# A graph attention layer on one core: another order for the lead-in and for the last places

## The chip, the cores and the metric

The kernel runs on one core of a Trainium2 chip. Its time is the device time of one execution in microseconds; every kernel is run several times, and the median counts. A profiled execution leaves a trace with the start and duration of each instruction on TensorE (PE, and PEld for its weight loads), VectorE (DVE), ScalarE (ACT), GpSimd (POOL) and SyncE (SP), and of the transfers. SP, ACT and POOL each issue transfers, and each has a queue of its own: q1 is SP's, q10 ACT's, q0 POOL's.

## The reference

One layer of attention over a graph, with a residual and a layer norm. There are 16 batches of 1024 nodes with 512 features, 8 heads of 64, and one adjacency matrix for all batches. It is sparse: node i has few neighbours, and the fewer the larger i is.

```python
def reference(x, adj, Wq, bq, Wk, bk, Wv, bv, Wo, bo):   # x (16,1024,512), adj (1024,1024) of 0 and 1
    q = (x @ Wq + bq).reshape(b, n, 8, 64)
    k = (x @ Wk + bk).reshape(b, n, 8, 64)
    v = (x @ Wv + bv).reshape(b, n, 8, 64)
    scores = jnp.einsum('bqhd,bkhd->bhqk', q, k) / 8.0
    scores = scores + (1.0 - adj)[None, None] * -1e9
    out = jnp.einsum('bhqk,bkhd->bqhd', softmax(scores), v).reshape(b, n, 512)
    return layernorm(x + out @ Wo + bo)
```

## The kernel before

**The sparse form.** The 1024 nodes are sorted by their number of neighbours into 8 tiles of 128 queries. For each tile the kernel knows how many keys a query has at most, and handles them in blocks: in a block every one of 128 rows has one query and one key. POOL gathers the 128 rows of k and v by an indirect transfer (`kvg`, L1230), DVE multiplies them with the queries (`qk`, L1251) and sums over each head (`s`, L1255), ACT takes the exponential (L1266), and ACT or DVE multiplies it with v (`pv`, L1276 and L1280). The blocks of one query are added on DVE (L1292) or, for the tiles with many keys, by TensorE with a matrix of zeros and ones (`sum`, L1301 and L1302). `normalise` divides (`o`, L1322), TensorE transposes (`poT`, L1336), ACT copies (`oT`, L1340), and `finish` multiplies with Wo (`po`, L790), adds the residual, and normalises the row (L1099 to L1121). A spilled tile's oT is stored and loaded back as `oTs`.

**The dense part.** For every pair of tiles TensorE transposes x (`pxT`, L748) and computes q (`pq`, L790, four passes of 128x512 per tile) and k and v together. For k and v of a pair, seven products stand in place of eight (L947: `x`, `p6`, `p7`, `z`, `p4`, of which x and z are built up in two steps), with sums T1 to T4 of the weights' quarters (B11, B21, B12, B22; L382 to L387 on DVE) and sums of x (L774 to L777). Only the first pair of batch 0 takes k and v in the plain way (`pk` and `pv`, L919), since T1 to T4 aren't there yet. The results are stored to memory, k and v by L840 and q by L822, from SP's queue. DVE adds up all v of a batch (`vsum`, a tile with one buffer; L851 for the first pair, L854 for the others), TensorE makes their mean (`pm`, L858), ACT copies it (L862) and SP stores it (L864): a query without neighbours gets the mean.

**The order.** The program is written out by a loop over places n, from −39 to the last block, and each engine keeps the order in which its instructions were written. At each place come the steps of the blocks n to n+8, then what `later(k, fn)` has put down for this place, then units of TensorE work: `fronts` is the list of dense units, each with a cost in microseconds, and as many are taken as a credit allows that grows by a share per place. `urgent` holds units that go in ahead of the list. At the end of a place `preps` take a step: generators, each started at a place of its own (`prep`), whose `yield` means "go on at the next place".

**The lead-in.** The places below 0 are the lead-in. `loads` issues the weights on ACT's queue, then zeros for the rows that nobody writes; `ranks` loads adj on POOL's queue, counts the neighbours on DVE (L451, L452) and ACT (L453), ranks the nodes (L485) and scatters them into `order` (L479); `pranks` (L497) is a transpose of the ranks. `checks` and `estimate` look at the degrees (`est`, L672; `poff`, L675), `more_ranks` makes tables for the merged tiles (L552 to L578) with small copies on SP's queue (L539 and L543), `lookups` translates keys to places. `bias_setup` makes the norms of the biases (L399 to L405), then the bias as columns, `bvb` (L415), and `pb3` (L419), which folds bv into bo. The first three tiles of x are loaded by SP before the loop, and each transposed tile issues the load of the third tile after it (`load_x`, L741). The units of TensorE begin with

```python
fronts += transpose_x(0, 0) + transpose_x(0, 1)
```

and go on with q of both tiles, the next two transposes, pk and pv.

**The last places.** While the last three blocks come, TensorE's list may hold a `finish` of a tile (eight passes with a bias row, L1078) between the last sums.

Of the kernel before, what the change touches and what calls it, by code (L numbers as in the profile page):

```python
# [10 lines left out]
F32 = mybir.dt.float32  # L11
# [3 lines left out]
OP = mybir.AluOpType  # L15
# [46 lines left out]
MORE_RANKS_AT = -12  # L62
# [11 lines left out]
P = 128  # L74
# [103 lines left out]
def kernel(  # L178
# [36 lines left out]
    nc = tc.nc  # L215
# [32 lines left out]
    def broadcast(t, v):  # L248
        nc.scalar.dma_start(t, bass.AP(tensor=v.tensor, offset=v.offset, ap=[[0, P], [1, D]]))

    def load_w(t, w):
        nc.scalar.dma_start(t, w.rearrange("(c p) e -> p c e", p=P))

    with ExitStack() as main:
# [6 lines left out]
        def fill_psum(name):  # L261
            return psum.tile([P, HALF], F32, tag="fill", name=name, bufs=4)
# [12 lines left out]
        nc.gpsimd.iota(placed, pattern=[[P, max(BLOCKS)]], base=1, channel_multiplier=1, allow_small_or_imprecise_dtypes=True)  # L275
        query = one.tile([P, NT], F32, name="query")
# [79 lines left out]
        def loads():  # L356

            load_w(W["q"], wq)
            broadcast(bq_bc, bq)
            nc.vector.tensor_scalar(bq_bc, bq_bc, scale, None, op0=OP.mult)  # L360
            yield

            B12[0] = work.tile([P, 2, D], F32, tag="kv", name="b12", bufs=5)
            load_w(B11, wk[0:HD2, :])
            load_w(B21, wk[HD2:D, :])
            load_w(B12[0], wv[0:HD2, :])
            load_w(B22, wv[HD2:D, :])
# [3 lines left out]
            for rows in solo_rows + pair_rows:  # L371
                for r in range(N, rows.shape[0], N + 1):
                    nc.scalar.dma_start(rows[r:r + 1, 0:D], zeros[0:1, 0:D])
            for i in range(1, ROWS):
                nc.scalar.dma_start(q_rows[i][ds(ONE_KEY * P, P), :], zeros[:, 0:D])
                if i % B >= PAIRED_FROM and not merged(i):
                    nc.scalar.dma_start(q_rows[i][0:P, :], zeros[:, 0:D])
            left = P - 8 * (B - PAIRED_FROM)
            nc.scalar.dma_start(more_rows[P - left:, :], zeros[0:left, 0:D])
# [14 lines left out]
        def bias_setup():  # L394
            bk_bc = work.tile([P, D], F32, tag="y", name="bk_bc", bufs=Y_BUFS)
            broadcast(bk_bc, bk)
            yield
# [8 lines left out]
            yield  # L406
            pb = fill_psum("pb")
# [8 lines left out]
            yield  # L416
# [25 lines left out]
        def later(k, fn):  # L442
            plan.setdefault(now[0] + k, []).append(fn)
# [11 lines left out]
        def ranks():  # L455
# [40 lines left out]
            pr = fill_psum("pranks")  # L496
            nc.tensor.transpose(pr[0:NT, 0:P], rank, ident)  # L497
# [5 lines left out]
            yield  # L503
            yield
# [31 lines left out]
        def more_ranks():  # L536
# [15 lines left out]
            nc.vector.tensor_scalar(steps, place[:, 0:n], float(spare), query[:, 0:1], op0=OP.mult, op1=OP.is_le)  # L552
            nc.vector.tensor_reduce(eighths, steps, axis=AX.X, op=OP.add)
            nc.vector.tensor_scalar(steps, place[:, 0:n], float(2 * spare), query[:, 0:1], op0=OP.mult, op1=OP.is_le)
# [23 lines left out]
            nc.vector.tensor_scalar(missing, missing, -NEG, None, op0=OP.mult)  # L578
            yield
# [7 lines left out]
        def lookups():  # L587
# [4 lines left out]
            for i, group in enumerate(groups):  # L592
                while i >= NT and i < len(groups) - 1 and len(SHORT) + i - NT not in listed:
                    yield
# [22 lines left out]
        shifts, looked = [], []  # L617
# [13 lines left out]
        def edges(t):  # L631
# [41 lines left out]
            yield  # L673
# [133 lines left out]
        def pair(b, j):  # L807
# [25 lines left out]
            def send(i):  # L833
# [8 lines left out]
                if R["sent"] == 2:  # L842
                    later(1, add_v)
                    if j == NT // 2 - 1:
                        later(2, lambda: urgent.append(mean_pe))
# [67 lines left out]
            if (b, j) == (0, 0):  # L913
# [12 lines left out]
                units = q0 + q1 + xt  # L926
# [55 lines left out]
            def s(i):  # L982
                return lambda: SX[b, j][i - 1]
# [3 lines left out]
            units += unit("p6", s(2), T2, True, out_w, None)  # L987
            units += q0
# [452 lines left out]
        prep.setdefault(BIAS_AT, []).append(bias_setup())  # L1441
        prep.setdefault(CHECKS_AT, []).append(checks())
# [5 lines left out]
        with tc.manual_schedule():  # L1448

            fronts += transpose_x(0, 0) + transpose_x(0, 1)  # L1450
# [19 lines left out]
            while n < total or plan or rest or urgent or done or finishing or spilled or lone_tiles or not guarded:  # L1470
# [53 lines left out]
                while credit > 0 or urgent:  # L1524
# [9 lines left out]
                    units = finishing or fronts  # L1534
# [55 lines left out]
```

## Time and profile before

| what | value |
|---|---|
| median of five runs | 1891.6 us (1887.18 to 1895.26) |
| profiled execution | 1895.35 us, its span 1893.4 us |
| granted TensorE clock | 0.986 on average |
| busy: PE, DVE, ACT, POOL | 1819.9, 1700.2, 1531.7, 1281.2 us |
| PE busy in 0 to 100, 100 to 200, 200 to 300 us | 88.52, 91.84, 100.00 us |
| DVE busy in the same | 74.99, 84.53, 85.18 us |
| PE busy in 1850 to 1893.4 us | 24.75 us |
| bytes moved, mean rate | 544.63 MB, 288 GB/s |

The times of the views count from the start of the span. A line of the timeline gives the start, the duration, the engine, the line of the kernel, the operation with its output and inputs, how many of them follow each other, and in brackets the idle time before and what ended it. PE's clock is throttled by the chip: where the granted clock is below 1.00, the same pass takes up to twice as long.

### The profile page before, as it was taken

The numbers are of one execution on the slowest core, as the hardware profiler recorded it, in microseconds if no ns is written. First come the engines' busy times: TensorE is split into PE (matmuls) and PEld (weight loads), VectorE is DVE, ScalarE is ACT, GpSimd is POOL, SyncE is SP. The second block draws the span as 40 slices with busy tenths as digits, with TensorE's granted clock in tenths as the row PEclk, the third lists the DMA queues.
The fourth block names the chain that finished last, engine by engine and source line by source line (L and its number), as shares of the span: only waits on it lengthen the run. The fifth ranks groups of instructions, "written<-read, shape, count | busy, mean of one in ns | idle before, by whom it ended". The sixth has DMA issues, their size and how long they took to land. (4 is left out here: it accounts for less than half of the span.)

```text
span 1893.4 us, 25101 instructions
## 1 busy us (share of the span) xinstructions
PE 1819.9 (96%) x5149; PEld 879.3 (46%) x5149; DVE 1700.2 (90%) x3484; ACT 1531.7 (81%) x6016; POOL 1281.2 (68%) x1189
## 2 busy tenths in 40 slices
PE   7989999999999999999999999999999999999996
PEld 3434444444545454444445444444445444444442
DVE  6888889999999999899899989899999989997874
ACT  3628869979788988889797978889898989886794
POOL 1357766777677677758677677767766777656774
PEclk9989999999999999999999999999999999999997
DMA  7357786988888988888889898998889898989893
GB/s 279 119 167 230 227 311 228 317 291 293 302 291 312 315 313 290 314 287 299 306 294 330 274 332 276 301 310 305 304 306 328 291 348 307 318 288 344 328 314 119
DMA packets 188149, 544.63 MB, mean 288 GB/s; under 512 B 32602, under 2 KB 32622, under 8 KB 187986
## 3 DMA queue, kind: packets, MB, share of 16 engines
q0 software_dynamic: 116400, 382.82, 60.2%
q1 hardware_dynamic: 68510, 154.30, 21.9%
q10 hardware_dynamic: 3076, 5.82, 0.9%
q14 instruction: 120, 0.98, 0.2%
q8 instruction: 43, 0.70, 0.1%
HBM read 419.52 MB, written 144.34 MB: 298 GB/s over the span
## 5 line engine op out<-in xcount | busy, mean ns | idle before, releaser
L1276 ACT ACTIVATE pv<-kvg,pv 128x64 f32<-128x64 f32 x3432 | 864.7, 340 | 0.0
L1230 POOL DMA_INDIRECT kvg<-kv_pair,place_row x462 | 533.6, 1155 | 246.9 <-ACT pv L1276 66.4
L790 PE MATMUL po<-wo,oT 128*128 128x512 f32 x816 | 385.2, 603 | 0.8 <-ACT oT L1340 0.8
L790 PE MATMUL pq<-wq,xT 128*128 128x512 f32 x792 | 370.4, 599 | 0.2 <-DVE q L821 0.2
L1255 DVE TENSOR_REDUCE s<-qk 128x8 f32<-128x512 f32 x530 | 360.3, 680 | 7.5
L1251 DVE TENSOR_TENSOR qk<-qt,kvg 128x512 f32<-128x512 f32 x434 | 296.6, 683 | 26.2 <-DMA kvg<-kv_pair,place_row 26.2
L947 PE MATMUL x<-b,xT 128*128 128x512 f32 x504 | 238.9, 597 | 0.8 <-ACT e L960 0.8
L947 PE MATMUL pp<-t,s 128*128 128x512 f32 x504 | 237.4, 593 | 1.5 <-DVE s L776 0.9
L790 PEld LDWEIGHTS po<-wo,oT 128*128 128x128 f32 x816 | 154.5, 193 | 169.9 <-issue 158.0
L1292 DVE TENSOR_TENSOR pv<-pv,pv 128x520 f32<-128x520 f32 x329 | 228.2, 693 | 0.7 <-ACT pv L1276 0.6
L790 PEld LDWEIGHTS pq<-wq,xT 128*128 128x128 f32 x792 | 149.4, 192 | 166.1 <-issue 154.8
L1266 ACT ACTIVATE pv<-s,absent 128x8 f32<-128x8 f32 x434 | 126.6, 294 | 85.4 <-DVE s L1255 84.0
L1001 POOL DMA_INDIRECT x<-in_x_dram,asked_row x120 | 134.4, 1120 | 87.5 <-PE pxT L748 39.5
L1125 POOL DMA_INDIRECT out_dram<-y,asked_row x129 | 146.3, 1134 | 35.6 <-issue 18.5
L800 ACT ACTIVATE sq_k<-kv 128x128 bf16<-128x128 f32 x512 | 150.9, 301 | 5.7 <-DVE kv L970 5.7
L947 PEld LDWEIGHTS x<-b,xT 128*128 128x128 f32 x504 | 94.8, 192 | 112.4 <-issue 106.1
L947 PEld LDWEIGHTS pp<-t,s 128*128 128x128 f32 x504 | 94.2, 190 | 112.9 <-issue 103.3
L1184 POOL DMA_INDIRECT qg<-q_rows,query_row x96 | 107.4, 1119 | 39.4 <-issue 22.0
L947 PE MATMUL z<-b,s 128*128 128x512 f32 x252 | 119.8, 598 | 6.6 <-DVE kv L975 6.6
L1029 POOL DMA_INDIRECT y<-in_x_dram,asked_row x93 | 104.0, 1118 | 27.4 <-issue 25.3
L947 PE MATMUL z<-t,s 128*128 128x512 f32 x252 | 118.6, 593 | 0.0
L947 PE MATMUL pp<-t,xT 128*128 128x512 f32 x252 | 118.4, 592 | 0.0
(276 smaller groups left out, 2764.0 us busy)
## 6 DMA issues: line engine op xcount, KB each, us to landing
kv_pair<-kv SPq DMA_DIRECT2D x98, 512.0 KB
q_rows<-q SPq DMA_DIRECT2D x106, 256.0 KB
qt<-q_rows SPq DMA_DIRECT2D x98, 256.0 KB
residual<-x SPq DMA_DIRECT2D x36, 256.0 KB
y<-residual SPq DMA_DIRECT2D x36, 256.0 KB
kv_rows<-kv SPq DMA_DIRECT2D x15, 512.0 KB
kvg<-kv_pair,place_row POOLq DMA_INDIRECT x462, 6.5
kv_pair<-kv SPq DMA_DIRECT2D x28, 256.0 KB
```

What stands on the lines that cost most here:

```text
L790: nc.tensor.matmul(p, lhs(c), w[:, c, :], start=(c == 0), stop=(c == NPAIR - 1))
L800: nc.scalar.activation(sq, s[:, ts(h, P)], AF.Square, scale=scale, accum_out=sums[:, h:h + 1])
L947: nc.tensor.matmul(R[bank], l[:, ts(c, P)], right[:, c, :], start=(first and c == 0), stop=(c == 1), skip_group_check=True,)
L1001: nc.gpsimd.indirect_dma_start(out=y, out_offset=None, in_=x_rows, in_offset=bass.IndirectOffsetOnAxis(ap=asked_row[:, t:t + 1], axis=0), ...
L1125: nc.gpsimd.indirect_dma_start(out=out_rows[b, t], out_offset=bass.IndirectOffsetOnAxis(ap=rows, axis=0), in_=y, in_offset=None, element_o ...
L1184: nc.gpsimd.indirect_dma_start(out=q, out_offset=None, in_=q_rows[b % ROWS], in_offset=bass.IndirectOffsetOnAxis(ap=rows, axis=0))
L1230: nc.gpsimd.indirect_dma_start(out=KG[n], out_offset=None, in_=rows, in_offset=bass.IndirectOffsetOnAxis(ap=(place_row if b else key_row)[ ...
L1251: nc.vector.tensor_tensor(QK[n], q, KG[n][:, 0:D], op=OP.mult)
L1255: nc.vector.tensor_reduce(S[n], QK.pop(n).rearrange("p (h d) -> p h d", d=HD), axis=AX.X, op=OP.add)
L1266: nc.scalar.activation(PV[n][:, D:], S.pop(n), AF.Exp, bias=bias)
L1276: nc.scalar.activation(pv[:, ts(h, HD)], v[:, ds(D + h * HD, HD)], AF.Copy, scale=pv[:, D + h:D + h + 1])
L1292: nc.vector.tensor_tensor(PV[b, t], PV[b, t], pv, op=OP.add)
```

## The change

The change leaves all arithmetic as it is, up to the order of additions of one bias, and moves these things:

- At the front, TensorE takes the transpose of tile 0 and its four q passes, then tile 1 and its passes. Wq comes in four loads of a quarter each. The loads of Wk and Wv go from ACT's queue to SP's, behind the first three tiles of x; the load of the fourth tile, x_3, stands behind them there.
- The ten stores of zeros go from ACT's queue to POOL's.
- `pranks` goes behind the ranked loads, by one place; `poff` comes three places after `est` in place of one, and `pb3` three after `bvb`.
- `more_ranks`, with its tables and small copies, starts at place 6 in place of −12. The norms, in a generator of their own (`bias_norms`), start at place 20. `ordinal`, a small iota, takes the place of `place` in the tables, whose buffer is given to something else by then, and `others_ready` holds the last group of the lookups back.
- `mean_pe` comes four places after the last pair's send in place of two, in every batch.
- In the first pair of a batch, the units stand in the order x, p6, transpose, x, p7, z, q of tile 0, transpose, p4, z; before, it was x, p6, q of tile 0, x, p7, both transposes, z, p4, z.
- In the last three places TensorE takes the sums alone; the finish of a tile that stood between them goes behind them. That tile's bias is added by DVE in place of a bias row on TensorE.

```diff
--- before.py
+++ after.py
@@ -59,7 +59,8 @@
 ADJ_AT = {-36: (0,), -35: (1, 2), -34: (3, 4), -33: (5,), -32: (6, 7)}
 CHECKS_AT = -27
 BIAS_AT = -8
-MORE_RANKS_AT = -12
+MORE_RANKS_AT = 6
+NORMS_AT = 20
 LOOK_FROM = -17
 REST_FROM = {7: -24, 6: -9}
 
@@ -273,6 +274,8 @@
         nc.gpsimd.iota(place, pattern=[[1, SPAN]], base=1, channel_multiplier=0, allow_small_or_imprecise_dtypes=True)
         placed = one.tile([P, max(BLOCKS)], F32, name="placed")
         nc.gpsimd.iota(placed, pattern=[[P, max(BLOCKS)]], base=1, channel_multiplier=1, allow_small_or_imprecise_dtypes=True)
+        ordinal = one.tile([P, B], F32, name="ordinal")
+        nc.gpsimd.iota(ordinal, pattern=[[1, B]], base=1, channel_multiplier=0, allow_small_or_imprecise_dtypes=True)
         query = one.tile([P, NT], F32, name="query")
         nc.gpsimd.iota(query, pattern=[[P, NT]], base=0, channel_multiplier=1, allow_small_or_imprecise_dtypes=True)
 
@@ -355,28 +358,26 @@
 
         def loads():
 
-            load_w(W["q"], wq)
+            for c in range(NPAIR):
+                nc.scalar.dma_start(W["q"][:, c, :], wq[ts(c, P), :])
             broadcast(bq_bc, bq)
             nc.vector.tensor_scalar(bq_bc, bq_bc, scale, None, op0=OP.mult)
-            yield
 
             B12[0] = work.tile([P, 2, D], F32, tag="kv", name="b12", bufs=5)
-            load_w(B11, wk[0:HD2, :])
-            load_w(B21, wk[HD2:D, :])
-            load_w(B12[0], wv[0:HD2, :])
-            load_w(B22, wv[HD2:D, :])
+            for t, w in ((B11, wk[0:HD2, :]), (B21, wk[HD2:D, :]), (B12[0], wv[0:HD2, :]), (B22, wv[HD2:D, :])):
+                nc.sync.dma_start(t, w.rearrange("(c p) e -> p c e", p=P))
             for _ in range(5):
                 yield
             load_w(W["o"], wo)
             for rows in solo_rows + pair_rows:
                 for r in range(N, rows.shape[0], N + 1):
-                    nc.scalar.dma_start(rows[r:r + 1, 0:D], zeros[0:1, 0:D])
+                    nc.gpsimd.dma_start(rows[r:r + 1, 0:D], zeros[0:1, 0:D])
             for i in range(1, ROWS):
-                nc.scalar.dma_start(q_rows[i][ds(ONE_KEY * P, P), :], zeros[:, 0:D])
+                nc.gpsimd.dma_start(q_rows[i][ds(ONE_KEY * P, P), :], zeros[:, 0:D])
                 if i % B >= PAIRED_FROM and not merged(i):
-                    nc.scalar.dma_start(q_rows[i][0:P, :], zeros[:, 0:D])
+                    nc.gpsimd.dma_start(q_rows[i][0:P, :], zeros[:, 0:D])
             left = P - 8 * (B - PAIRED_FROM)
-            nc.scalar.dma_start(more_rows[P - left:, :], zeros[0:left, 0:D])
+            nc.gpsimd.dma_start(more_rows[P - left:, :], zeros[0:left, 0:D])
             nc.vector.tensor_scalar(before, place[:, 0:P], -1.0, query[:, 0:1], op0=OP.add, op1=OP.is_gt)
             yield
             nc.vector.tensor_tensor(T1, B12[0], B11, op=OP.subtract)
@@ -391,9 +392,10 @@
             nc.scalar.dma_start(bias_rows[NPAIR:, :], bk.rearrange("(c p) -> c p", p=P))
             nc.scalar.dma_start(bv_rows, bv.rearrange("(c p) -> c p", p=P))
 
-        def bias_setup():
+        def bias_norms():
             bk_bc = work.tile([P, D], F32, tag="y", name="bk_bc", bufs=Y_BUFS)
             broadcast(bk_bc, bk)
+            yield
             yield
             n4 = small.tile([P, NPAIR], F32, name="bk_norms", bufs=1)
             nc.vector.tensor_tensor(bk_bc, bk_bc, bk_bc, op=OP.mult)
@@ -404,6 +406,8 @@
             nc.vector.tensor_reduce(n8, bk_bc.rearrange("p (h d) -> p h d", d=HD), axis=AX.X, op=OP.add)
             nc.vector.tensor_reduce(bq_norm, n8, axis=AX.X, op=OP.max)
             yield
+
+        def bias_setup():
             pb = fill_psum("pb")
             nc.tensor.transpose(pb[:, 0:2 * NPAIR], bias_rows, ident[:2 * NPAIR, :2 * NPAIR])
             nc.tensor.transpose(pb[:, 2 * NPAIR:3 * NPAIR], bv_rows, ident[:NPAIR, :NPAIR])
@@ -413,7 +417,8 @@
             nc.vector.tensor_copy(bv_col, pb[:, 2 * NPAIR:3 * NPAIR])
             bvb = work.tile([P, NPAIR, P], F32, tag="y", name="bvb", bufs=Y_BUFS)
             nc.vector.tensor_copy(bvb, bv_col[:, :, None].to_broadcast([P, NPAIR, P]))
-            yield
+            for _ in range(3):
+                yield
             pb = fill_psum("pb3")
             for c in range(NPAIR):
                 nc.tensor.matmul(pb, bvb[:, c, :], W["o"][:, c, :], start=(c == 0), stop=(c == NPAIR - 1))
@@ -493,14 +498,14 @@
             nc.vector.tensor_copy(rank_row[:, NT - 1:NT], rank[:, NT - 1:NT])
             scatter(NT - 1)
             yield
-            pr = fill_psum("pranks")
-            nc.tensor.transpose(pr[0:NT, 0:P], rank, ident)
             nc.sync.dma_start(ranked[:, 2:, :], order[2 * P:, :].rearrange("(t p) c -> p t c", p=P))
             nc.sync.dma_start(ranked[0:LONE, 0, :], order[0:LONE, :])
             nc.sync.dma_start(ranked[LONE:, 0, :], order[LONE + P:2 * P, :])
             nc.sync.dma_start(ranked[:, ONE_KEY, :], order[LONE:LONE + P, :])
 
             yield
+            pr = fill_psum("pranks")
+            nc.tensor.transpose(pr[0:NT, 0:P], rank, ident)
             yield
             nc.vector.tensor_copy(asked_row[:, 0:NT], ranked[:, :, 0])
             known.append(True)
@@ -549,9 +554,9 @@
             eighths, upper, lower, sixteenths, odd = (w[:, i:i + 1] for i in range(5))
             steps = w[:, 6:6 + n]
             shifts.extend((upper, odd))
-            nc.vector.tensor_scalar(steps, place[:, 0:n], float(spare), query[:, 0:1], op0=OP.mult, op1=OP.is_le)
+            nc.vector.tensor_scalar(steps, ordinal[:, 0:n], float(spare), query[:, 0:1], op0=OP.mult, op1=OP.is_le)
             nc.vector.tensor_reduce(eighths, steps, axis=AX.X, op=OP.add)
-            nc.vector.tensor_scalar(steps, place[:, 0:n], float(2 * spare), query[:, 0:1], op0=OP.mult, op1=OP.is_le)
+            nc.vector.tensor_scalar(steps, ordinal[:, 0:n], float(2 * spare), query[:, 0:1], op0=OP.mult, op1=OP.is_le)
             nc.vector.tensor_reduce(sixteenths, steps, axis=AX.X, op=OP.add)
             nc.vector.scalar_tensor_tensor(odd, sixteenths, -2.0, eighths, op0=OP.mult, op1=OP.add)
             nc.vector.tensor_scalar(upper, query[:, 0:1], LONE - 0.5, None, op0=OP.is_gt)
@@ -576,6 +581,7 @@
             nc.vector.tensor_scalar(missing, rows, 0.0, None, op0=OP.is_lt)
             nc.vector.scalar_tensor_tensor(key_row[:, at + 1:at + 3], missing, NO_ROW, rows, op0=OP.mult, op1=OP.max)
             nc.vector.tensor_scalar(missing, missing, -NEG, None, op0=OP.mult)
+            others_ready.append(True)
             yield
 
             for h in range(HEADS):
@@ -590,7 +596,7 @@
             groups += [[first[t] + i for i in range(BLOCKS[t])] for t in range(len(SHORT), NT)]
             groups.append(list(range(at, at + 4)))
             for i, group in enumerate(groups):
-                while i >= NT and i < len(groups) - 1 and len(SHORT) + i - NT not in listed:
+                while i >= NT and not (others_ready if i == len(groups) - 1 else len(SHORT) + i - NT in listed):
                     yield
                 for g in group:
                     nc.gpsimd.indirect_dma_start(
@@ -614,7 +620,7 @@
 
                 later(3, copy)
 
-        shifts, looked = [], []
+        shifts, looked, others_ready = [], [], []
 
         def checks():
             for t in range(NT):
@@ -670,7 +676,8 @@
                 nc.vector.tensor_tensor(check[:, 2 * NT + 1:2 * NT + 2], ranked[:, t, 1:2], st[:, 0:1], op=OP.subtract)
 
             nc.vector.tensor_scalar(deg, ranked[:, t, 1:2], -float(K), 0.0, op0=OP.add, op1=OP.max)
-            yield
+            for _ in range(3):
+                yield
             po = fill_psum(f"poff_{t}")
             nc.tensor.matmul(po[:, 0:1], before, deg, start=True, stop=True)
             yield
@@ -842,7 +849,7 @@
                 if R["sent"] == 2:
                     later(1, add_v)
                     if j == NT // 2 - 1:
-                        later(2, lambda: urgent.append(mean_pe))
+                        later(4, lambda: urgent.append(mean_pe))
 
             def add_v():
                 kv = [KV.pop((b, t))[:, D:] for t in tt]
@@ -923,7 +930,8 @@
 
                     return [(PRODUCT, lambda c=c: unit(c), None) for c in range(NPAIR)]
 
-                units = q0 + q1 + xt
+                q0, q1 = ([(cost, fn, lambda i=i: (0, i) in XT) for cost, fn, _ in q] for i, q in enumerate((q0, q1)))
+                units = q0 + transpose_x(0, 1) + q1 + xt
                 for i in range(2):
                     units += plain(i, f"pk_{i}", lambda: B11, B21, out_k)
                 for i in range(2):
@@ -985,6 +993,8 @@
             units = []
             units += unit("x", lambda: a(0, 0), B11, True, out_e, None)
             units += unit("p6", s(2), T2, True, out_w, None)
+            if j == 0:
+                q0, q1, xt = xt[:1], q0 + xt[1:], []
             units += q0
             units += unit("x", lambda: a(0, 1), B21, False, lambda: out_k(0, R["x"]), "e")
             units += unit("p7", s(3), T3, True, out_g, None)
@@ -1439,6 +1449,7 @@
         for t, n in REST_FROM.items():
             prep.setdefault(n, []).append(edges(t))
         prep.setdefault(BIAS_AT, []).append(bias_setup())
+        prep.setdefault(NORMS_AT, []).append(bias_norms())
         prep.setdefault(CHECKS_AT, []).append(checks())
         preps = [loads(), ranks()]
         prep.setdefault(start[B - 1] + 8, []).append(guard())
@@ -1447,7 +1458,7 @@
         prep.setdefault(LOOK_FROM, []).append(lookups())
         with tc.manual_schedule():
 
-            fronts += transpose_x(0, 0) + transpose_x(0, 1)
+            fronts += transpose_x(0, 0)
             fronts_by = []
             for b in range(B):
                 for j in range(NT // 2):
@@ -1521,7 +1532,8 @@
                     reload(*spilled.pop(0), reloads)
                     reloads, last_reload = reloads + 1, n
                 first_unit = True
-                while credit > 0 or urgent:
+                last_sums = total - 3 <= n < total
+                while credit > 0 and not last_sums or urgent:
                     if urgent and not (first_unit and fronts):
                         urgent.pop(0)()
                         continue
@@ -1531,7 +1543,7 @@
                     ):
                         finishing = finish(*done.pop(0))
                         last_finish = n
-                    units = finishing or fronts
+                    units = [] if last_sums else finishing or fronts
                     if not units:
                         if urgent:
                             urgent.pop(0)()
```

## The prediction

> **What bounds the kernel now.** I read the page first, then time windows, then TensorE's waits, then its timeline where a window showed a hole. On the page:
>
> ```profile
> PE 1819.9 (96%) x5149; PEld 879.3 (46%) x5149; DVE 1700.2 (90%) x3484; ACT 1531.7 (81%) x6016; POOL 1281.2 (68%) x1189
> PE   7989999999999999999999999999999999999996
> PEclk9989999999999999999999999999999999999997
> ```
>
> PE is busy 1819.9 of 1893.4 us, so all idle time together is 73.5 us, and the slices put it at both ends: in the first, the third and the last, where the clock row also dips. The windows (columns: busy time of PE, its weight loads, DVE, ACT, POOL; granted clock; DMA share; GB/s):
>
> ```profile
> 0.00:20.00 20.00, 13.27 (x36) 6.69 (x36) 3.99 (x6) 5.96 (x10) 7.67 (x28) 1.00 0.89 340
> 20.00:40.00 20.00, 17.21 (x40) 7.56 (x41) 19.59 (x21) 9.43 (x30) 0.00 (x0) 1.00 0.75 281
> 100.00:120.00 20.00, 17.50 (x48) 7.71 (x47) 14.69 (x42) 5.38 (x21) 6.88 (x8) 0.83 0.43 142
> 120.00:140.00 20.00, 14.68 (x36) 6.42 (x35) 18.56 (x53) 7.59 (x33) 15.43 (x16) 0.91 0.77 239
> 200.00:300.00 100.00, 100.00 (x287) 49.02 (x286) 85.18 (x172) 75.90 (x310) 71.58 (x66) 1.00 0.79 264
> 1860.00:1880.00 20.00, 15.78 (x35) 7.45 (x34) 7.53 (x32) 9.13 (x17) 10.20 (x11) 0.74 0.34 129
> ```
>
> Four holes can be had: 0 to 40 (transfers), 100 to 120, 120 to 140, and the tail; between them PE is full. TensorE's waits (total, times, longest) name them:
>
> ```profile
> PE sum L1301 <- DVE pv L1280: 14.1, 6, 3.8
> PE z L947 <- DVE kv L975: 6.6, 6, 2.4
> PE pxT L748 <- DMA x<-in_x_dram: 6.6, 2, 3.9
> PE pm L858 <- DVE vsum L854: 6.0, 5, 1.9
> PE pb L419 <- DVE bvb L415: 5.3, 1, 5.3
> ...
> PE poff L675 <- DVE est L672: 2.5, 1, 2.5
> PE pk L919 <- DMA b<-in_L_gnn_Wk_dram: 2.4, 1, 2.4
> ```
>
> The timeline shows what an idle stretch costs behind itself (start, duration, instruction, [idle before]):
>
> ```profile
> 107.49 0.59 PE L675 MATMUL poff<-est,before 128*128 128x1 f32 x2 [2.50 <-DVE est L672]
> 107.94 2.05 PE L790 MATMUL pq<-wq,xT 128*128 128x512 f32 x2
> ...
> 135.08 5.09 PE L419 MATMUL pb<-wo,bvb 128*128 128x512 f32 x8 [5.32 <-DVE bvb L415]
> ...
> 1873.37 6.34 PE L790 MATMUL po<-wo,oT 128*128 128x512 f32 x8 [0.79 <-ACT oT L1340]
> ```
>
> A pass of 128x512 takes 0.43 us at full clock (eight take 3.43). After the 2.50 us of idle, pq, pm and x up to 114.67 took 7.18 us where their passes are worth 3.63: 3.55 lost. After the 5.32, pb took 4.93 for 3.43: 1.5 lost. The last po lost 2.9.
>
> **The parts, step by step.** The sum is made against the profiled execution, 1895.35 us (span 1893.4 and 1.95 around it); it stands 3.75 above the median, 1891.6.
>
> *Removed from PE between 100 and 140.* poff goes three places later (a place is about 3.3 us: 530 score reductions on DVE fill some 1760 us): −2.50 −3.55. pb3 stands three places behind bvb: −5.32 −1.5. pranks goes behind the ranked loads: −1.28. Together −14.15 if nothing else is late.
>
> *Added at the front.* x_3's load was alone on SP's queue; now Wk and Wv, 2.1 MB, stand ahead of it there, and PE must transpose x_3 before the first pk. Before, up to 28 us 10.01 MB went over all queues at about 410 GB/s. If all of x (1.0), Wq, bq, Wk, Wv (3.4) and adj (4.2) is ahead, x_3 lands at 2.5 + 8.6/0.41 = 23.5 us; if adj's queue takes only half, near 20; with 1 MB of the zeros, which are now also on POOL's queue, 26. I take 24.5. PE, whose pq_0 now starts as each quarter of Wq lands, is through pq_1 at about 16. It then waits some 8.5 us in place of 2.69 + 2.40, and starts cold: the sixteen pq passes at 8.60, cold too, took 8.54 instead of 6.9. Then pk and x_3's transpose begin at 25 and end near 33, where before pk ended at 27.5: +5.5; the 0.52 and 0.68 that PE waits for DVE at 36.8 and 44.7 absorb some, +4.9 remains. Each microsecond of x_3's landing counts in full: landing at 20 adds 0.4, at 26 adds 6.4. The net for PE would be −14.15 + 4.9 = −9.3.
>
> On the Trainium skill, "TensorE: Matmul & The Clock Gate", Part 1, says that the gate closes after about 3.4 us of idle and opens after as much work. Here the 2.50 us of idle was followed by half rate, and idle of 3.57 us at 802 was not; the rows decide. By the rule, the 3.55 would not be there to win.
>
> The same skill, "DMA: Bandwidth & Descriptors", section "Issuing engines are not separate DMA queues", speaks against moving Wk and Wv from ACT's queue to SP's: all transfers run on the same 16 engines, and only issue time is saved. The 410 GB/s at which the lead-in sits agrees; the move would be worth nothing by it.
>
> *DVE comes next.* The two tables (L552 to L578) and the norms (L399 to L405) cost 2.1 + 3.05 + 1.24 = 6.4 us on DVE between 123 and 130, ahead of bvb and of the first block's qk (134.94). They go behind the first blocks, into 150 to 300, where DVE has 14.8 us idle in each 100: nothing, or 6.4 if that idle time is no cover. DVE thus gains 6.4 and PE 9.3; at 153.96 z already waits 0.34 for DVE's kv. It will wait 0.34 + 9.3 − 6.4 = 3.2. **Lead-in −6** (−10.6 with x_3 at 20 and DVE not late; −4.6 at 26; 0 if a new cold stretch follows the z wait).
>
> *Queues passed.* ACT loses ten zero stores, 6.5 us of blocked issue before key_of at 35.99; that engine is idle half of that window: nothing. POOL takes them where it sits idle 38 us before the scatter L479: nothing; without that cover ten issues of about 0.6 us (adj's row), 6. SP issues the four weight loads, and the 19 small table copies go from before the first mean store to behind the first blocks: the mean store at 114.41 stood behind them, and the first gather (116.42) waited. That gains up to 3 us for the gathers, which the qk above needs only after DVE; nothing. Norms' eight squares on ACT: 8 x 0.61, in a window where ACT is 76% busy.
>
> *Middle.* pm comes two places (6.6 us) later in every batch, and on j = 0 pairs more work lies between the two z. Five pm waits are 6.0, one for ACT 1.4, the later z waits 6.3: 13.7 in all. DVE is 94 to 97% busy there, so most of a wait given up comes back at the next consumer: I take a fifth, **−2.5**, from −6 to +3 (DVE pays 6.4 if the tables are not covered).
>
> *Tail.* In before, four sum pairs, a po of oTs (3.16 + 0.38 + 1.88, half of it cold) and two more sum pairs alternate, and o is ready at 1870.99. Now the sums run first: the last pv of DVE ends at 1862.4, so the last sum ends near 1865, o at 1867. po_3 fills PE until 1869, poT and its copy end at 1870, and the last po takes 3.43 at full clock or 6.34 cold: it ends at 1873.5 or 1876.4, against 1879.7. Two rows are now normalised one after the other, +0.9. **Tail −5** (−2.4 cold, −6 at best).
>
> Sum −6 − 2.5 − 5 = −13.5, 1881.9 from the profiled execution, 1878.1 from the median. The 3.75 between them is probably in part the same middle waits, so I take **1880**.
>
> **Rivals.** *The pace is DVE's and the gathers'.* DVE waits 31.2 us for gathers (kvg), and sum waits 14.1 for DVE's pv; if these set the course from the first block on, the lead-in's gain becomes more of the same waits, and only the tail remains: −5, 1886.6. For it: DVE 94 to 97%. Against: qk starts 6 us earlier too, and PE has no idle time at 200 to 300. *Weights and x_3 come early* (20 us): lead-in −10.6, in all −17, 1874. For it: one queue less competes. Against: 410 GB/s is already drawn. *The tail stays cold*: −2.4 there, about 1882.5. *DVE waits behind the later pm* (the slower side): vsum has one buffer, so DVE's first vsum add (L851) of the next batch cannot write before PE has read the old one in pm, and DVE executes in order, with the qk and pv of the blocks behind it. In batch 1 pm ends at 212.3 and that add is at 221.7; 6.6 us later leaves 2.8. If PE lags DVE by more than that in most of the 15 changes of batch, each costs about a place's 3.3: from five of them (16.5) the −13.5 is gone; at about six it is +6, 1897. Against: in batches 0 and 2 the add came 19.5 us after pm's end and over 30 after its start (131.3; 302.4 and 335.5).
>
> **How the numbers follow.** Forecast 0.45, pace of DVE 0.20, early x_3 0.13, cold tail 0.10, vsum 0.12. A measurement tells about 0.3%, 5.7 us, from no change: the bound for faster is 1885.9. Faster: 0.45 x 0.93 + 0.20 x 0.4 + 0.13 + 0.10 x 0.8 = 0.71. Slower: 0.12 x 0.75 + 0.20 x 0.1 = 0.11. The rest, 0.18, is the same. The range goes from lead-in −10.6, middle −6 and tail −6 (1869) to the DVE case with the uncovered tables (1886.6 + 6.4, less the 2 that the tail may still bring: 1891). That leaves out the vsum case and little else.
>
> **What would show it.** Right: no idle before poff and pb3 and full clock from 100 to 160; x_3's transpose waiting for its load until 23 to 26; a z wait of about 3 us near 148; sums back to back at 1865 less the shift, and a last po of 3.4 us. Wrong: DVE's L858 (the old L851) waiting for pm; sum waits over 20 us; DVE's first qk not earlier than 131; x_3 after 28.

## The result and the profile after

The changed kernel takes 1883.31 us in the median of 37 runs, the kernel before 1890.78 in 63: a ratio of 0.996 (95% interval 0.9951 to 0.9968), 7.5 us less. The forecast was 1880, with 1869 to 1891 as its range, from 1891.6. The profiled execution of the changed kernel took 1885.03 us, its span 1882.8. Lines of the changed kernel stand a few numbers later in the file (L748 is L755, L790 is L797, L1251 is L1261); tail_alone has the numbers of before, and in the other experiments' kernels they differ from the changed kernel's by one or two.

The windows of the changed kernel (columns as before):

```profile
20.00:40.00 20.00, 13.80 (x29) 6.54 (x30) 17.52 (x19) 8.51 (x22) 3.60 (x7) 0.74 0.69 254
100.00:120.00 20.00, 18.73 (x49) 7.81 (x48) 18.94 (x50) 4.67 (x20) 11.20 (x11) 1.00 0.40 128
120.00:140.00 20.00, 19.79 (x62) 9.76 (x61) 17.90 (x39) 6.84 (x28) 14.91 (x14) 1.00 0.68 222
```

The two holes between 100 and 140 are filled: PE went from 17.50 and 14.68 us to 18.73 and 19.79, at full clock. A new one stands between 20 and 40, 13.80 in place of 17.21, and the clock fell to 0.74 there; between 0 and 20 PE is busy 11.37 us in place of 13.27. TensorE's timeline names the hole, and its echo on DVE:

```profile
26.20 1.08 PE L755 MATMUL pxT<-ident,x 128*128 128x128 f32 x4 [8.13 <-DMA x<-in_x_dram]
27.08 9.32 PE L926 MATMUL pk<-b,xT 128*128 128x512 f32 x16
...
51.68 1.95 PE L478 MATMUL pkeys<-ident,keys 128*128 128x128 f32 x16
...
115.98 0.28 PE L682 MATMUL poff<-est,before 128*128 128x1 f32 x2
...
131.44 3.60 PE L424 MATMUL pb<-wo,bvb 128*128 128x512 f32 x8
...
148.69 1.98 PE L955 MATMUL z<-b,s 128*128 128x512 f32 x4 [0.54 <-DVE kv L983]
...
1864.11 3.60 PE L797 MATMUL po<-wo,oT 128*128 128x512 f32 x8
```

```profile
54.29 1.28 DVE L490 SCALAR_TENSOR_TENSOR keys<-key_of,key,place 128x1024 f32<-128x1024 f32 x1 [3.43 <-ACT key_of L480]
```

pkeys and the start of the ranks in the kernel before:

```profile
44.68 2.05 PE L473 MATMUL pkeys<-ident,keys 128*128 128x128 f32 x16 [0.68 <-DVE keys L469]
47.39 1.28 DVE L485 SCALAR_TENSOR_TENSOR keys<-key_of,key,place 128x1024 f32<-128x1024 f32 x1 [0.96 <-ACT key_of L475]
```

x_3's transpose waits 8.13 us for its load. The sixteen pk passes behind it take 9.32 us, where the sixteen warm pv passes that follow take 7.03: 2.29 lost, some five passes at half rate ("cold"). pkeys, which stood at 44.68 before, comes at 51.68. The ranks (L490, L485 before) wait for ACT's copy of pkeys (key_of), and start at 54.29; before they started at 47.39. At the other places the forecast is seen: poff and pb3 without a wait, and a warm last po, 3.60 for 6.34.

TensorE's waits, total, times and longest:

```profile
PE pxT L755 <- DMA x<-in_x_dram: 12.9, 2, 8.1
PE sum L1311 <- DVE pv L1290: 9.1, 9, 1.7
PE poT L1346 <- DVE o L1332: 4.6, 4, 2.0
PE z L955 <- DVE kv L983: 4.0, 4, 2.0
PE pp L955 <- DVE s L783: 2.9, 4, 1.6
```

No pm is in the list any more, and z fell from 6.6 to 4.0. Waits for o, s, q, y and g are new or longer: from 150 us on all of TensorE's waits add up to 37.8 us, 40.3 before.

**Where the gain is.** DVE sums the scores of 530 blocks (L1255 before) in the same sequence in every version, so the k-th of them is a landmark. This table gives how much earlier (−) a trace reaches it than the trace of before does, and how much earlier the span ends.

| kernel | first block | block 40 | block 160 | last block | end of span | from the last block to the end (us) |
|---|---|---|---|---|---|---|
| before, time of it (us) | 135.7 | 291.9 | 676.7 | 1858.9 | 1893.4 | 34.5 |
| changed | −1.9 | −3.6 | −1.9 | −5.0 | −10.6 | 28.9 |
| tail_alone | −1.0 | −0.3 | −0.6 | −9.4 | −15.2 | 28.7 |
| no_tail | −0.9 | −2.5 | −1.1 | −3.1 | −5.5 | 32.1 |
| tables_early | +2.2 | +0.1 | +0.1 | −6.4 | −9.0 | 31.9 |
| x3_first | −7.1 | −8.7 | −8.6 | −14.9 | −17.6 | 31.8 |
| x3_first_again | −7.1 | −8.7 | −8.8 | −16.1 | −18.8 | 31.8 |
| x3_adj_early | −10.0 | −11.6 | −12.1 | −19.3 | −24.8 | 28.9 |
| x3_no_gaps_again | −3.5 | −4.6 | −4.5 | −8.0 | −13.5 | 28.9 |
| x3_old_middle | −3.2 | −5.8 | −5.3 | −9.9 | −12.6 | 31.7 |

Up to block 160 it is steady: the two traces of x3_first, on two chips, agree to 0.2 us there, and tail_alone, which has the instructions of before up to its last places, is 0.6 from it. Behind that single executions drift apart: the same tail_alone is 9.4 us ahead of before at the last block. The windows from 700 us to the last block, of before and of tail_alone, say in what:

```profile
700.00:1858.90 1158.90, 1126.15 (x3203) 545.37 (x3201) 1066.95 (x2159) 987.10 (x3915) 811.83 (x733) 0.99 0.88 306
700.00:1849.50 1149.50, 1117.75 (x3200) 541.40 (x3198) 1066.27 (x2157) 986.61 (x3912) 807.65 (x732) 1.00 0.89 309
```

DVE's time is the same to 0.7 us, but PE's is 8.4 us longer in before, for three passes more (1.3 us), and at a lower clock. In before six windows of 20 us have a granted clock of 0.91 there (from 900, 1115, 1195, 1550, 1720 and 1810 us), in tail_alone the first of them alone. The trace of before was a long execution (1895.35 against a median of 1890.78), and its losses lie late. So the lead-in is read here from the landmarks up to block 160, and the whole from medians and ratios.

**Where part of the gain goes.** The changed kernel's 3.6 us at block 40 are 1.9 at block 160, and no_tail's 2.5 are 1.1; x3_first and tables_early lose nothing there. Between these landmarks a po of TensorE waits 1.97 us for DVE's y. Every version of the table with the new middle has this wait (1.97 to 1.99); at the same place before has 0.45 and 0.80 us. The rows of the changed kernel and of x3_first:

```profile
301.27 5.40 PE L797 MATMUL po<-wo,oT 128*128 128x512 f32 x8 [1.97 <-DVE y L1109]
```

```profile
296.15 3.70 PE L798 MATMUL po<-wo,oT 128*128 128x512 f32 x8 [1.98 <-DVE y L1110]
```

After the same wait the eight passes run cold in the changed kernel and in no_tail (5.40 us), and warm in tables_early and in the versions with x_3 first (3.70): the 1.7 us between them are what the two lost. Why the clock falls in some traces and not in the others is not shown.

### The profile page after: what moved, and what is told of

Its sections match the earlier page's. It is cut to its first block, busy times and chain, and to the rows that moved or that the text cites. A ratio compares the mean times of both kernels' runs of the same rounds, so it can differ in the third digit from the quotient of the medians.

```text
span 1882.8 us, 25104 instructions
## 1 busy us (share of the span) xinstructions
PE 1812.9 (96%) x5148; PEld 875.5 (46%) x5148; DVE 1701.4 (90%) x3485; ACT 1530.7 (81%) x6016; POOL 1271.2 (68%) x1201
## 4 chain that ended last, share of the span: by engine, by line
PE 26%; DVE 10%; ACT 7%; issue 4%; DMA 3%; POOL 1%; POOLq 0%; DVEq 0%; ACTq 0%
PE po L797 7%; PE pq L797 5%; PE pp L955 4%; ACT pv L1286 4%; PE z L955 3%; PE x L955 3%; DVE qk L1261 2%; DMA kvg<-kv_pair,place_row 2%; DVE s L1265 2%; PE poT L1346 1%; DVE pv L1302 1%; PE sum L1312 1%; PE sum L1311 1%; PE pxT L755 1%; DVE y L1110 1%
## 5 line engine op out<-in xcount | busy, mean ns | idle before, releaser
L1240 POOL DMA_INDIRECT kvg<-kv_pair,place_row x462 | 524.8, 1136 | 244.5 <-ACT pv L1286 69.6
L797 PE MATMUL po<-wo,oT 128*128 128x512 f32 x816 | 381.4, 599 | 4.0 <-ACT oT L1350 2.0
L797 PE MATMUL pq<-wq,xT 128*128 128x512 f32 x792 | 368.3, 596 | 2.4 <-ACT xT L759 2.0
L1261 DVE TENSOR_TENSOR qk<-qt,kvg 128x512 f32<-128x512 f32 x434 | 296.8, 684 | 23.9 <-DMA kvg<-kv_pair,place_row 23.8
L797 PEld LDWEIGHTS po<-wo,oT 128*128 128x128 f32 x816 | 154.0, 192 | 170.2 <-issue 154.2
L797 PEld LDWEIGHTS pq<-wq,xT 128*128 128x128 f32 x792 | 147.9, 191 | 168.0 <-issue 151.4
```

The lines of the kernel that those rows point to most:

```text
L797: nc.tensor.matmul(p, lhs(c), w[:, c, :], start=(c == 0), stop=(c == NPAIR - 1))
L1240: nc.gpsimd.indirect_dma_start(out=KG[n], out_offset=None, in_=rows, in_offset=bass.IndirectOffsetOnAxis(ap=(place_row if b else key_row)[ ...
L1261: nc.vector.tensor_tensor(QK[n], q, KG[n][:, 0:D], op=OP.mult)
```

## The experiments

**The parts one by one.** Theory A: what the lead-in gains arrives at the end, the parts add up. Theory B: the middle uses it up, and only the tail remains. tail_alone is the kernel before with this edit, no_tail is the changed kernel without it:

```diff
-                while credit > 0 or urgent:
+                last_sums = total - 3 <= n < total
+                while credit > 0 and not last_sums or urgent:
...
-                    units = finishing or fronts
+                    units = [] if last_sums else finishing or fronts
```

> The kernel before, with the one edit that TensorE takes only sums in the last three places. Theory A (the parts add up: what the lead-in gains arrives at the end): the traces of before and after are 5.0 us apart at the last block's score sum and 10.6 at the end, so this edit is worth 5.6 us: 1885.2, ratio 0.997. Theory B (the lead-in's gain is used up in the middle, the tail is all that the change brings): 7.5 us, 1883.3, ratio 0.996. In the trace the last po is preceded by five pairs of sums without another pass between them, and it takes about 3.4 us in place of 6.3.

Measured: 1886.88 against 1890.36, ratio 0.9978 (0.9960 to 0.9997): some 4 us, and the interval holds A's 0.997 as well as B's 0.996. In tail_alone's timeline the last two po are warm:

```profile
1854.46 3.60 PE L790 MATMUL po<-wo,oTs 128*128 128x512 f32 x8
...
1859.69 3.60 PE L790 MATMUL po<-wo,oT 128*128 128x512 f32 x8
```

From the last block's score to the end of the span 28.7 us pass here (1878.2 less 1849.5), 28.9 in the changed kernel, 34.5 in the kernel before. But the edit does not always bring these 5.6 to 5.8 us. In tables_early, both traces of x3_first and x3_old_middle, which have it too, 31.7 to 31.9 us pass, hardly less than the 32.1 of no_tail, which does not. There the last sums run at half rate, after the same wait. One of them in the changed kernel and in x3_first:

```profile
1856.15 0.70 PE L1311 MATMUL sum<-pv,sums 128*128 128x256 f32 x2 [0.95 <-DVE pv L1290]
```

```profile
1846.24 1.22 PE L1312 MATMUL sum<-pv,sums 128*128 128x256 f32 x2 [0.94 <-DVE pv L1291]
```

The last po is warm in all of them, 3.60 us. So the last places take two courses some 3 us apart, and a trace or a median can differ by that without the lead-in having any part in it.

> The changed kernel without the last-sums edit: all of the lead-in, the later pm and the j = 0 order, and the tail of before. Theory A: the first qk was 1.9 us earlier in the changed kernel, so 1.9 us remain of 7.5, 1889, ratio 0.999. Theory B: nothing remains, 1890.8, ratio 1.000. Either way the last po takes over 6 us again, cold.

Measured: 1886.73, ratio 0.9968 (0.9948 to 0.9988). The last po is cold again, 5.40 us. By the ratios each half brings 4 to 6 us (by the medians 3.5 and 3.6); the intervals are too wide to see whether the halves add up to 0.996 exactly. B, that nothing remains without the tail, lies outside, and so, just, does A's 0.999.

**x_3 in front of the weights.** The dearest term of the forecast's lead-in was x_3's load behind 2.1 MB. This edit lets the loop issue x_3 first:

```diff
             nc.vector.tensor_scalar(bq_bc, bq_bc, scale, None, op0=OP.mult)
+            yield
 
             B12[0] = work.tile([P, 2, D], F32, tag="kv", name="b12", bufs=5)
...
-            for _ in range(5):
+            for _ in range(4):
                 yield
```

> The changed kernel with the loads of Wk and Wv issued one place later, so that x_3 stands ahead of them on SP's queue. Both theories: x_3 lands by 13 us in place of 26.2, the idle time of 8.1 us before its transpose shrinks to a wait of 3 to 5 us for Wk, and pkeys moves from 51.7 to about 45. Theory A: the rank chain (first L490 at 54.3) and the first qk (133.0) come 5 to 7 us earlier, and the whole execution with them: 1877, ratio 0.993. Theory B: the first qk is as much earlier, but the time stays at 1883, ratio 0.996.

Measured: 1876.65 beside 1890.36, ratio 0.9915 (0.9890 to 0.9941). Once more on another chip:

> The kernel with x_3 ahead of Wk and Wv once more, so that the three kernels beside it are compared with it on one chip. It measured 0.9915 of before elsewhere; theory A expects that again, 0.990 to 0.994.

1878.41 beside 1889.5, ratio 0.9954 (0.9935 to 0.9973). The two intervals overlap only from 0.9935 to 0.9941; both medians lie 11 to 14 us under before, 5 to 7 under the changed kernel. The timeline of x3_first:

```profile
17.82 1.04 PE L756 MATMUL pxT<-ident,x 128*128 128x128 f32 x8
18.70 1.88 PE L927 MATMUL pk<-b,xT 128*128 128x512 f32 x4
21.21 5.42 PE L927 MATMUL pk<-b,xT 128*128 128x512 f32 x12 [0.64 <-DMA b<-in_L_gnn_Wk_dram]
...
45.53 3.07 PE L479 MATMUL pkeys<-ident,keys 128*128 128x128 f32 x16 [3.18 <-DVE keys L475]
```

Both tiles are transposed without a wait, pk waits 0.64 us for Wk, and the ranks start at 49.27. The first block comes 5.2 us earlier than in the changed kernel, block 40 5.1 us, block 160 6.7 (1.7 of it the cold po), and the median 5 to 7 us. Against before, the 8.7 us of block 40 are still there at block 160 in both traces. Theory A holds up to there: the start of the blocks is passed on one to one. B's 0.996 lies outside the first run's interval, though not outside the second's; the landmarks speak against it.

**The weights' queue.** The same stall can be taken away by giving Wk and Wv back to ACT's queue (`load_w(t, w)` in place of `nc.sync.dma_start`).

> The changed kernel with the loads of Wk and Wv back on ACT's queue, behind the four loads of Wq; x_3 is alone on SP's queue again. Theory A (x_3's place is what costs, not the queue of the weights): x_3 lands by 13 us, pk begins with Wk at 19 to 22, and the time is that of x_3 first, 1877, ratio 0.992, or some 2 us more where ACT's xT copies wait behind the blocked issues. The rival, that the weights are faster on SP's queue: pk begins after 24 and the time stays at 1883, ratio 0.996.

Measured: 1926.6 beside 1928.1, ratio 0.999 (0.9956 to 1.0024). This and three others ran on a chip on which the kernel before took 1928.1 us and DVE's waits were partly for nothing that the trace shows (some 25 us "issue" in weights_act); differences under 0.4% can't be read there, and the time settles nothing. The lead-in can be read:

```profile
19.62 1.04 PE L755 MATMUL pxT<-ident,x 128*128 128x128 f32 x8
20.49 7.03 PE L926 MATMUL pk<-b,xT 128*128 128x512 f32 x16
```

x_3 isn't waited for, and pk runs without a gap from 20.49: on ACT's queue Wk is there by 22 us, and on SP's by 21.21 (above). These rows show no difference that the queue makes to the weights; x_3's place behind them made one. The first block comes 3.0 us earlier than in the changed kernel.

**Tables and norms ahead of the blocks again** (`MORE_RANKS_AT = -12`, `NORMS_AT = -11`):

> The changed kernel with the tables at place -12 again and the norms at place -11, so their 6.4 us on DVE and the 19 small copies on SP lie ahead of the first blocks as before. Theory A: DVE's first qk moves from 133.0 to about 138 (6.4 less the idle time that DVE has there, 1.3), and the end with it, less what the blocks get back in 150 to 300: +3 to +5 against the changed kernel, 1887, ratio 0.998. Theory B: the 6.4 us are paid in either place and the time is as with the change, 1883, ratio 0.996.

Measured: 1887.35, ratio 0.9981 (0.9963 to 1.0000), 4.0 us more than the changed kernel's median. The first block is 4.1 us later than in the changed kernel, block 40 3.7. The landmarks show A, and the size that was expected. By time it is less sure: the intervals of the two kernels (0.9963 to 1.0000 and 0.9951 to 0.9968) overlap, and in its trace tables_early takes 3.0 us more in the last places, where its sums run cold.

**The three places before poff and pb3.** In x_3 first, both back to one place:

```diff
-            for _ in range(3):
-                yield
+            yield
             pb = fill_psum("pb3")
...
-            for _ in range(3):
-                yield
+            yield
             po = fill_psum(f"poff_{t}")
```

> x_3 first, and poff and pb3 again one place after est and bvb as in the kernel before. Theory A1 (TensorE's holes between 100 and 140 set the lead-in): the waits of 2.5 and 5.3 us and the cold passes behind them come back, some 8 to 12 us, and the first blocks with their k and v come later: 1884 to 1888, ratio 0.996. Theory A2 (DVE's rank chain sets the first blocks, and TensorE has room): the two waits come back in the trace, the first qk and the end stay: 1877, ratio 0.992.

It gave 0.9972 (0.9932 to 1.0012) on the chip of 1928.1 us, not to be told from either. The second run stood beside x3_first_again:

> x_3 first with poff and pb3 one place after est and bvb. The first look showed a wait of 4.0 us before poff and none before pb3, and a first qk 3.4 us later than with x_3 first. Theory A1 (TensorE's hole counts): 3 to 4 us and a few cold passes more than x_3 first, +5, 0.994. Theory A2 (DVE's chain has the say): as x_3 first, 0.9915.

Measured: 1886.49, 8.1 us over x3_first_again, ratio 0.9983 (0.9968 to 0.9998) against its 0.9954 (0.9935 to 0.9973). The timeline of x3_no_gaps_again:

```profile
109.28 0.38 PE L681 MATMUL poff<-est,before 128*128 128x1 f32 x2 [3.79 <-DVE est L678]
109.52 2.39 PE L954 MATMUL pp<-t,s 128*128 128x512 f32 x4
111.71 3.19 PE L954 MATMUL z<-t,s 128*128 128x512 f32 x4
...
126.98 3.60 PE L424 MATMUL pb<-wo,bvb 128*128 128x512 f32 x8
```

poff's wait is back, and the eight passes behind it take 5.58 us where four take 1.88 warm: some 1.8 lost. The first block is 3.6 us later, block 40 4.1, block 160 4.3. So TensorE's hole counted (A1). But pb3 waits for nothing, though it stands one place behind bvb: with the tables and norms out of the way, the three places there bring nothing. In tables_early, which has the three places and the tables ahead, pb3 doesn't wait either, but a pass ahead of it does:

```profile
130.73 3.42 PE L955 MATMUL pp<-t,s 128*128 128x512 f32 x4 [3.40 <-DVE s L783]
```

The hole of 5.3 us thus came from the tables and norms on DVE; the three places alone move it to another consumer.

**The middle.** pm two places after the send again (x3_mean2), the old order in a batch's first pair (x3_j0_old), and both (x3_old_middle), in x_3 first:

> x_3 first, and pm two places after the last send as before. The prediction gave the middle 2.5 us for this and the j = 0 order together. Theory C (waits only change their name): pm waits for vsum come back, some 6 us in all, the waits for g, q and y go down by as much, time 1877, ratio 0.992. Theory D (the later pm is worth its waits): 1881 to 1883, ratio 0.995.

> x_3 first, and in the first pair of each batch the old order of units (x, p6, q, x, p7, both transposes, z, p4, z). Theory C: z waits for kv come back to some 6 us, others fall, time 1877, ratio 0.992. Theory D: 1879 to 1883, ratio 0.994. The other side: the old order is the better one by the waits for s, g and q that the trace of the changed kernel has new (some 7 us), 1872, ratio 0.989.

Both ran on the chip of 1928.1 us: 0.9945 (0.9912 to 0.9978) and 0.9980 (0.9949 to 1.0012). x3_first itself was not run on that chip, so neither says what its edit does; inconclusive.

> x_3 first with the old middle: pm two places after the last send and the old order of units in the first pair of each batch. The prediction's term for both was 2.5 us. Theory C (a wait given up in the middle comes back under another name): same time as x_3 first within 2 us, with pm and z waits of some 12 us in the trace and fewer others; 0.9915. Theory D: 3 to 8 us more, 0.994 to 0.996. Other side: the old middle is 3 us faster, 0.990.

Measured: 1882.57, 4.2 us over x3_first_again; ratio 0.9962 (0.9944 to 0.9980) against 0.9954, so by the intervals no difference is shown. Waits and timeline of x3_old_middle:

```profile
PE pm L866 <- DVE vsum L862: 10.1, 6, 4.2
PE z L956 <- DVE kv L984: 6.1, 5, 2.4
```

```profile
110.53 1.87 PE L866 MATMUL pm<-vsum,mean 128*1 128x512 f32 x2 [4.21 <-DVE vsum L862]
```

The longest pm wait stands in the lead-in, at batch 0, where the changed order has none; the first block is 3.9 us later, block 40 2.9, block 160 3.5. From 150 us on all of TensorE's waits are 39.9 us, against 38.8 in x3_first_again: the pm and z waits are traded for others, as theory C said, and what the new middle brings with x_3 first it brings in the lead-in.

**A better kernel.** In x_3 first DVE was idle from 13.9 to 18.0 and then full up to the ranks, for whose keys TensorE waited 3.18 us. One tile of adj can go into that gap:

```diff
-ADJ_AT = {-36: (0,), -35: (1, 2), -34: (3, 4), -33: (5,), -32: (6, 7)}
+ADJ_AT = {-37: (0,), -36: (1,), -35: (2,), -34: (3, 4), -33: (5,), -32: (6, 7)}
```

> x_3 first, and DVE takes the first tile of adj before the second tile's q: DVE sat idle 4.1 us there, from 13.9 to 18.0, and from then on it was full until the ranks, for whose keys TensorE waited 3.2 us at 45.5. Theory A (the first blocks hang on DVE's chain through the ranks, and the end on the first blocks): pkeys 2.5 us earlier, near 43, the ranks and the first qk with it, and the time 2.5 us under that of x_3 first, 0.990 of before. Theory B2 (the chain waits later for the ranked loads or the gathers anyway): the pkeys are as much earlier, the first qk and the time are not.

Measured: 1872.43 beside 1889.5, ratio 0.9922 (0.9900 to 0.9944), 6.0 us under x3_first_again by the medians. pkeys of x3_adj_early:

```profile
43.66 2.05 PE L479 MATMUL pkeys<-ident,keys 128*128 128x128 f32 x16 [1.57 <-DVE keys L475]
```

The first block and block 40 are 2.9 us earlier than with x_3 first, as expected from 2.5, and block 160 3.3 to 3.5. The remaining 3 us of the medians are those of the last places in the traces: 28.9 us in x3_adj_early, 31.8 in x3_first_again, and the edit has no part in them that is shown. It has the lowest median of all versions; its ratio is not under the 0.9915 of x3_first's first run.

## Why the prediction was right, point by point

**Direction, range and mechanism.** Faster was right, and 1883.31 lies in the range; but the range reaches to 1891 and would have held no change (1890.78) as well. The size, 7.5 us, is two thirds of the 11.6 that the forecast gave. The holes and the tail went as forecast; the way of x_3's delay and the middle did not.

**The holes at 100 to 140 (−14.15).** They went as forecast, and the clock stayed at 1.00. The share-out was wrong at pb3: of −6.8, nothing belonged to its three places once the tables are moved (x3_no_gaps_again), and with the tables ahead the places only hand the wait on (tables_early). With x_3 first, poff's three places are worth 3.6 us at the first block and 4.1 at block 40.

**x_3 behind the weights (+4.9).** The landing was forecast at 24.5 and the wait at 8.5; it was 26.20 and 8.13. (The sum's 410 GB/s is a little high: from 2.5 us on, where it starts, the kernel before has 384 GB/s up to 28 us, and 8.6 MB at that rate end at 24.9.) The term was too small all the same. pk began at 27.08, not 25, and ended at 36.4, not 33; pq behind it came 7.95 us late (46.53 for 38.58). The step that failed is the next: "DVE thus gains 6.4 and PE 9.3". DVE's chain was taken as not touched by x_3. But the ranks need pkeys from PE and its copy from ACT, so PE's delay went on into DVE: pkeys 7.0 us late, ranks 6.9, `est` 7.1 (114.36 for 107.28). That ate the 6.4 us: the first block came only 1.9 us earlier, and x3_first gives the missing 5.2 back. The bounds of the lead-in have a flaw of the same kind: they count x_3's landing one for one, though by the sum the z waits for DVE, not for PE.

**Lead-in −6.** At the z where the two chains were weighed the trace shows −5.3 (148.69 for 153.96), at the first block −1.9, at block 40 −3.6. The z fitted by luck: the forecast has it wait 3.2 us for a DVE that is 6.4 earlier, but DVE's first block was 1.9 earlier, and z waited 0.54. The sign of an error that the forecast had named, a first qk not earlier than 131, did show: 133.01.

**Tables and norms behind the blocks (nothing, or 6.4).** Moving them back costs 4.1 us at the first block and 3.7 at block 40, so by block 40 hardly any of the 6.4 was paid, as it should be if the idle time of DVE there was cover.

**Middle −2.5.** Nothing of it is seen, and the traces of the changed kernel and of no_tail have a loss in its place: a new wait of 1.97 us for y and 1.7 us of cold passes behind it. pm's 7.4 us and 2.6 of z's are gone, but TensorE's waits from 150 us on sum to 37.8 us in the changed kernel and 36.5 in tail_alone, which has the old middle. "Most of a wait given up comes back at the next consumer" was right, and all of it would have been nearer than four fifths. The later pm may have brought something in a place that the forecast did not look at: batch 0's pm, in the lead-in, waits 4.21 us in x3_old_middle and not at all in x3_first.

**Tail −5.** By tail_alone's ratio it is worth about 4, by the traces 5.6 where the last sums run warm and 2.6 to 2.8 where they run cold. The last po was warm, as forecast; that the sums ahead of it might be cold was not in the forecast.

**The sum.** In the changed kernel's trace −3.6 at block 40, +1.7 up to block 160 and −5.6 for the tail make −7.5, the number that was measured. That it comes out so exactly is luck, since the tail's 5.6 stands on one trace of before and on the warm course. The forecast's surplus is the lead-in's 2.4 and the middle, 2.5 us that did not come and 1.7 that were lost.

**The rivals.** The pace of DVE and the gathers is spoken against by x3_first, x3_adj_early and x3_no_gaps_again: what the first blocks gain or lose is still there at block 160, and the medians move the same way. The early x_3 (20 us) did not come about with the weights ahead of it. DVE has no wait for pm in its list, so the vsum rival did not show.

**Clock and queues.** In the Trainium skill, "TensorE: Matmul & The Clock Gate", Part 1, sets the bound for a cold restart at about 3.4 us of idle. The 8.13 and 3.79 us here were followed by cold passes, which agrees; the 2.50 of before was too, and so was the 1.97 of the changed kernel's po, which does not. The 1.98 of the same po in x3_first was not. "DMA: Bandwidth & Descriptors", section "Issuing engines are not separate DMA queues", says that all queues share the engines. This agrees with Wk, which is there by 21.21 us on SP's queue (x3_first) and by 22 on ACT's (weights_act). That section says nothing of the order within one queue, and that order is what cost here.

## What to carry to other kernels

When a transfer is moved to another queue, look at what then stands behind it there, and follow that one's consumer through every engine: a late x tile stopped TensorE for 8 us, and because the ranks' keys pass over TensorE, DVE's chain, which looked independent, was 7 us late too. In a lead-in, weigh the change at the first block of the steady part and not at a wait on the way, and then once more some hundreds of microseconds later. Behind the lead-in, the waits between the two busiest engines mostly changed their names here, and a new one cost more than its length where the clock fell behind it. A landmark that every version passes in the same sequence shows a shift of 3 us in one trace, where medians need many runs, as long as the clock has taken the same course up to it.

## What was not expected of the hardware

Single executions of the same instructions drifted 8.8 us apart between block 160 and the last block (−0.6 to −9.4 in tail_alone against before), though they agreed to 0.6 up to there; from 700 us on TensorE is busy 8.4 us longer in one, for nearly the same passes, with six dips of the clock against one in the other. After the same wait, 1.97 to 1.99 us at the po behind block 40 or 0.92 to 0.96 at the last sums, the passes were cold in some traces and warm in others. On one of the chips the kernel before took 1928.1 us in place of some 1890, with DVE waits that the trace puts down to "issue" and "remote".
